# Loading convolution taps one by one on SyncE, early x loads between batches, and embedding scalings on ScalarE in a two-layer graph kernel

## The chip, the core and the metric

The kernel runs on one core of a Trainium2 chip, in one launch. The metric is the device time of that launch in microseconds. A core has TensorE (PE: matrix products, with weight loads shown as PEld), VectorE (DVE), ScalarE (ACT), GpSimd (POOL) and SyncE (SP). Each runs its own instructions in order, and waits on semaphores for the others. Transfers are issued from SP, ACT or POOL and are carried out by 16 DMA engines.

## What is computed

`x` is 128 x 128 x 256 (batch, node, channel), `adj` 128 x 128 x 128, all float32. Two layers, each added to its input:

```python
# layer 0
h = relu(layernorm(x))
hc = relu(bn1(conv1x1(h)))
x_conv = relu(bn2(conv17(hc)) + h)            # 17 taps along the nodes, 256 -> 256 channels
s = h @ w_se.T + b_se                         # embedding, 3 wide
A = exp(-dist(s, s)) * adj
x_nmp = A @ relu(h @ w_msg.T + b_msg)
x = x + gru(concat(x_conv, x_nmp), h)
# layer 1, on the first 25 nodes
h = relu(layernorm(x))
norm_w = softmax(fusion_w)                    # 5 groups of nodes
for g, idx in enumerate(GROUPS):
    out_g = graph_conv(graph_conv(h[:, idx], adj_g, W1[g], b1[g]), adj_g, W2[g], b2[g])
    fused[:, idx] += norm_w[g] * out_g
x = x + fused
```

## The kernel before

The batch of 128 is cut into 32 quads of four matrices. The 17-tap convolution is done in a frequency domain: stage a (`stage_a`, lines 368 to 419) loads a quad of x, normalises it, transposes it (`hTa`), does the 1x1 convolution (`pc`) and the forward transform (`pf`) into `X`; stage b (line 478 on) multiplies the 40 frequencies of 64 matrices by transformed weights `wf`; stage c (line 658 on) transforms back and does the gated unit. Stages a and b run once for each of two batches of 16 quads. Stage c runs over all 32 quads, together with layer 1.

The transformed weights come from the taps. `load_taps(n)` (lines 427 to 434) loads a quarter of `conv2_w` into a buffer `wt` (two of these): tap t of the quarter's rows goes to the partitions t, 32 + t, 64 + t and 96 + t. `tap_weights` (lines 436 to 463) multiplies by a constant (`pw`), copies into `ws` and stores to `wfd` in DRAM from POOL. This runs beside stage a of the first batch. The quarter n + 1 is loaded while quarter n is worked on, at its first step (for n = 0 at its fourth), and a new load waits for the buffer's last reader on TensorE.

x quads are loaded by SP in `load_x` (line 360, four transfers of 128 KB), into four buffers `xa`; the statistics (`st`, line 267, `mv`, line 268) and the normalisation (line 275) follow on VectorE, with a power on POOL (line 270) between. SP also loads the tap quarters, the late constants (`load_late`, lines 250 to 253), `wf`, and later everything that stage c reads.

Beside stages a and b, from the end of `tap_weights` on, `early(q)` works out the neighbour part of quad q (`neighbours`, line 575 on): the embedding (`pse`), four scalings of it into `ef` (lines 586 and 589), their product `lr`, the messages (`pm`), the adjacency (`pd`, `aT`) and the sum (`px`). In the second batch, `fold_gates` (lines 305 to 326) loads and combines the gate weights.

Layer 1 (`setup_1`, `rows`, `prepare`, `block`) works in eight blocks of 16 matrices. The end of a block is `turn` (transpose back), `gather` (the second adjacency product) and `fuse` (the weighted sum over groups by the matrix `s2w`, added to `x1`), for four quads each; then four stores on POOL (line 1094).

The order of all instructions is fixed when the program is built: the pieces are generators, and an `Order` picks the lane with the least work done for its weight. A `yield a, b` says that the piece did `a` us of TensorE work and wants `b` us before its next step. No engine reorders at run time.

Of the kernel before, what the change touches and what calls it, by code (L numbers as in the profile page):

```python
# [9 lines left out]
FP = mybir.dt.float32  # L10
AF = mybir.ActivationFunctionType
ALU = mybir.AluOpType
# [195 lines left out]
def kernel(ctx: ExitStack, tc: tile.TileContext, x, adj, consts, vecs, w_se, conv1_w,  # L208
# [24 lines left out]
    def c(name):  # L233
        a, b = CAT[name]
        return cst[:, a:b]
# [13 lines left out]

    def load_late():  # L250

        nc.sync.dma_start(out=wse, in_=w_se.rearrange("(k p) o -> p k o", p=P))
        nc.sync.dma_start(out=cst[:, CFIRST:], in_=consts[:, CFIRST:])

    scl, sft = {}, {}
    brz = cp.tile([P, 4], FP, name="brz")
    wse9 = wp.tile([P, 2, WIDE], FP, name="wse9")
# [70 lines left out]
    def fold_embedding():  # L328
# [9 lines left out]
                                       op0=ALU.mult, op1=ALU.add)  # L338
        yield 1.5, 0.0

    lab, turn = ExitStack(), []
# [24 lines left out]
    def stage_a(q):  # L368
        ab = LATE["ab"]
        for n in range(q, min(q + 2, (q // BQ + 1) * BQ)):  # L370
            if n not in XA:
                load_xa(n)
                if n == q:
                    yield 0.0, 14.0 if q > BQ else 6.0
        if q not in MOM:
            MOM[q] = moments(XA[q], "a")
            yield 0.0, 3.0
            normalize(XA[q], XA[q], *MOM[q])
            yield 0.0, 2.0
# [12 lines left out]
        nc.gpsimd.dma_start(out=hTd[q], in_=hT)  # L392
        h1 = ab.tile([P, GB, D], FP, tag="h1", name=f"h1{q}")
        for h in range(2):
            pc = ptmp.tile([P, 2, D], FP, tag="tmp", name=f"pc{q}_{h}")
            for i in range(2):
                for k in range(2):
                    nc.tensor.matmul(pc[:, i], hT[:, k, (2 * h + i) * N:(2 * h + i + 1) * N],  # L398
                                     c1w[:, k], start=(k == 0), stop=(k == 1))
            s = slice(2 * h, 2 * h + 2)  # L400
            nc.vector.tensor_tensor(h1[:, s], pc, brow[:, None, :].to_broadcast([P, 2, D]),
                                    ALU.add)
            nc.scalar.activation(h1[:, s], h1[:, s], AF.Relu)
            yield 1.75, 2.8 * h
        for h in range(2):
            for k in range(2):
                pf = ptmp.tile([P, 2, D], FP, tag="tmp", name=f"pf{q}_{k}_{h}")
                for i in range(2):
                    nc.tensor.matmul(pf[:, i, :F * NB], h1[:, 2 * h + i, k * P:(k + 1) * P],  # L409
                                     fwd, start=True, stop=True)  # L410
                g0 = (q % BQ * GB + 2 * h) * NB
                dst = X[:, k, :, g0:g0 + 2 * NB].rearrange("p f (g b) -> p f g b", b=NB)
                src = pf[:, :, :F * NB].rearrange("p g (f b) -> p f g b", b=NB)
                if (k, h) == (0, 0):
                    nc.vector.tensor_copy(dst, src)  # L415
# [10 lines left out]

    def load_taps(n, *engines):

        wt = tw.tile([P, 16, D], FP, tag="wt", name=f"wt{n}")
        src = conv2_w.rearrange("(r n i) t o -> n t r i o", r=4, n=4)[n]  # L430
        for r in range(4):
            engines[r % len(engines)].dma_start(out=wt[32 * r:32 * r + 16], in_=src[:16, r])
        engines[0].dma_start(out=wt[16::32], in_=src[16])
        wts.append(wt)

    def tap_weights():

        yield 0.0, 16.0
        for n in range(4):
            for m in range(8):  # L440
                if m == (0 if n else 3) and n < 3:
                    load_taps(n + 1, nc.sync, nc.gpsimd)
                if (n, m) == (2, 4):
                    load_late()
                if m % 2 == 0:
                    ws = tw.tile([P, 4, 4, D], FP, tag="ws", name=f"ws{n}_{m}", bufs=3)
# [21 lines left out]
        LATE["wn"] = wg.tile([P, 7, 2, P], FP, name="wn")  # L468
        LATE["wh"] = wg.tile([P, 7, 1, P], FP, name="wh")
        LATE["io"] = near.enter_context(tc.tile_pool(name="io", bufs=2, reuse_waits="tile"))  # L470
        LATE["fr"] = near.enter_context(tc.tile_pool(name="fr", bufs=1, reuse_waits="tile"))
        LATE["wmsg"] = LATE["fr"].tile([P, 2, D], FP, name="wmsg")
        LATE["bmsg"] = LATE["fr"].tile([P, D], FP, name="bmsg")
# [4 lines left out]
    def stage_b(bat):  # L478
# [29 lines left out]
        for f in range(NF + 1):  # L508
            if f + 3 <= NF:
                load_w(f + 3)  # L510
            if f < NF:
                add(f + 1)
            y = xf.tile([P, 2, D], FP, tag="y", name=f"y{bat}_{f}")
            pa = pgat.tile([P, 2, D], FP, tag="gat", name=f"pa{bat}_{f}")
            for s in range(2):
# [59 lines left out]
    def neighbours(q, hT, ad, xm):  # L575
# [6 lines left out]
                                 hT[:, k, j * N:(j + 1) * N], start=(k == 0), stop=(k == 1))  # L582
        ef = LATE["fr"].tile([P, 4, N], FP, tag="ef", name=f"ef{q}")
        for i in range(4):
            if i % 2 == 0:
                nc.vector.tensor_scalar(ef[:, i], pse[:, :N], emb[:, i:i + 1], embb[:, i:i + 1],
                                        op0=ALU.mult, op1=ALU.add)
            else:
                nc.scalar.activation(ef[:, i], pse[:, :N], AF.Identity, scale=emb[:, i:i + 1],
                                     bias=embb[:, i:i + 1])  # L590
        lr = LATE["fr"].tile([P, 2, N], FP, tag="lr", name=f"lr{q}")
        nc.vector.tensor_tensor(lr, ef[:, 0::2], ef[:, 1::2], ALU.mult)
        yield 0.5, 0.0
# [277 lines left out]
    def setup_1():  # L871
# [6 lines left out]
            tc.tile_pool(name="l2", bufs=2, reuse_waits="tile"))  # L878
        b2s = pool.tile([NG, D], FP, tag="dd", name="b2s")
        nc.sync.dma_start(out=b2s, in_=b2)  # L880
        fus = pool.tile([P, NG], FP, name="fus")
        nc.sync.dma_start(out=fus, in_=fusion_w.partition_broadcast(P))
        for n in range(2):
            load_w1(n)
        S["w2"] = weight(pool, W2, [P, 5, 4, D], "g (k p) o -> p g k o", "w2", nc.sync)
# [4 lines left out]
        for t in (*r4, S["yz"][:, 0], S["yz"][:, 1], S["b1"]):  # L890
            nc.gpsimd.memset(t, 0.0)
            yield 0.0, 4.0

        fmx = pool.tile([P, 1], FP, name="fmx")
        nc.vector.reduce_max(fmx, fus, axis=mybir.AxisListType.X)
        nc.vector.tensor_scalar(fus, fus, fmx, None, op0=ALU.subtract)  # L896
        nc.scalar.activation(fus, fus, AF.Exp)
        fsm = pool.tile([P, 1], FP, name="fsm")
        nc.vector.reduce_sum(fsm, fus, axis=mybir.AxisListType.X)
        nc.vector.reciprocal(fsm, fsm)  # L900
        nc.vector.tensor_scalar(fus, fus, fsm, None, op0=ALU.mult)
        nc.vector.tensor_mul(fus, fus, c("grp"))
        wrow = pool.tile([P, 1], FP, name="wrow")
        nc.vector.reduce_sum(wrow, fus, axis=mybir.AxisListType.X)
        s2w = S["s2w"] = pool.tile([P, 2 * WIDE], FP, name="s2w")
        nc.vector.tensor_scalar(s2w, c("s2"), wrow, None, op0=ALU.mult)
# [95 lines left out]
    def block(blk):  # L1002
        while not (blk in P_DONE and blk - 1 in B1_DONE):
            yield 0.0, 0.5
        pool, yz, b2row, s2w = S["pool"], S["yz"], S["b2row"], S["s2w"]
        w2, ac, r4 = S["w2"], S["ac"][blk % 2], S["r4"][blk % 2]

        for q in range(QS):
# [48 lines left out]
        def turn(q):  # L1057
            pz = ptmp.tile([P, 2, D], FP, tag="tmp", name=f"pzt{blk}_{q}")
            for a in range(2):
                for cc in range(2):  # L1060
                    b0 = q * GB + 2 * a
                    nc.tensor.transpose(
                        pz[:, a, cc * P:(cc + 1) * P],
                        yz[:, cc, b0:b0 + 2, :].rearrange("p s r -> p (s r)"), ident)
            zt = zts[q] = pool.tile([P, 2, D], FP, tag="zt", name=f"zt{blk}_{q}", bufs=3)
            nc.scalar.activation(zt, pz, AF.Copy)

        def gather(q):
# [10 lines left out]
        def fuse(q):  # L1079
            zt = zts.pop(q)  # L1080
            pf = ptmp.tile([P, D], FP, tag="tmp", name=f"pfu{blk}_{q}")
            for a in range(2):
                nc.tensor.matmul(pf[a * 2 * WIDE:(a + 1) * 2 * WIDE], s2w, zt[:, a],
                                 start=True, stop=True)
            nc.vector.tensor_add(x1[:, q], x1[:, q], pf)

        for what, q in ((turn, 0), (turn, 1), (turn, 2), (gather, 0), (gather, 1), (fuse, 0),
                        (turn, 3), (gather, 2), (fuse, 1), (gather, 3), (fuse, 2), (fuse, 3)):
            what(q)
            if (what, q) == (gather, QS - 1):  # L1090
                B1_DONE.add(blk)
            yield {turn: 0.45, gather: 0.9, fuse: 0.5}[what], 0.5
        for j in range(GB):
            nc.gpsimd.dma_start(
                out=out[blk * SB:(blk + 1) * SB, :WIDE].rearrange("(q j) n c -> j n q c", j=GB)[j],
                in_=x1[j * WIDE:(j + 1) * WIDE])
        F_DONE.add(blk)


# [5 lines left out]
    load_xa(2)  # L1105
    fold()
    beside = Lane([tap_weights()] + [early(q) for q in range(NQ)])
    gates = Lane([fold_gates()], weight=0.5)
    for bat, (during_a, during_b) in enumerate(((0.66, 0.5), (0.2, 0.65))):
        if bat:  # L1110
            take_turn("ab", 2, reuse_waits="tile")
# [58 lines left out]
```

## Time and profile before

| | us |
|---|---|
| median of three runs (2089.95 to 2099.69) | 2099.61 |
| the profiled execution, its own time | 2107.02 |
| the span in its trace | 2105.2 |
| stage a, first batch, with the tap weights | 0 to about 180 |
| stage b, first batch | about 210 to 372 |
| stage a, second batch | about 372 to 530 |
| stage b, second batch | about 535 to 707 |
| stage c and layer 1 | about 710 to 2105 |

The page gives busy time by engine, the span in forty slices, the transfer queues, the chain of work that ended last, the costliest groups and the transfers. Windows give the same busy times for any stretch. Of the transfers that matter here the list says:

```profile
xa<-in_x SPq DMA_DIRECT2D x128, 128.0 KB, 5.2
...
wt<-in_conv_w SPq DMA_DIRECT2D x8, 256.0 KB, 9.5
wt<-in_conv_w POOLq DMA_DIRECT2D x8, 256.0 KB, 11.8
...
wt<-in_conv_w SPq DMA_DIRECT2D x3, 64.0 KB
```

The columns are tile and source, issuing queue, count, size of one, and the median time from issue to landing. A quarter of the taps is four transfers of 256 KB and one of 64 KB, and SP and POOL share them.

### The profile page before, as it was taken

The numbers are of one execution on the slowest core, as the hardware profiler recorded it, in microseconds if no ns is written. First come the engines' busy times: TensorE is split into PE (matmuls) and PEld (weight loads), VectorE is DVE, ScalarE is ACT, GpSimd is POOL, SyncE is SP. The second block draws the span as 40 slices with busy tenths as digits, with TensorE's granted clock in tenths as the row PEclk, the third lists the DMA queues.
The fourth block names the chain that finished last, engine by engine and source line by source line (L and its number), as shares of the span: only waits on it lengthen the run. The fifth ranks groups of instructions, "written<-read, shape, count | busy, mean of one in ns | idle before, by whom it ended". The sixth has DMA issues, their size and how long they took to land.

```text
span 2105.2 us, 31050 instructions
## 1 busy us (share of the span) xinstructions
PE 2045.2 (97%) x11316; PEld 1657.3 (79%) x11316; DVE 1181.8 (56%) x2775; ACT 686.8 (33%) x1543; POOL 725.5 (34%) x902
## 2 busy tenths in 40 slices
PE   7978999999999999999999999999999999999998
PEld 5656888789888788787878877878787787878875
DVE  6754544786544455655654565565565655654642
ACT  4643222344222333323232232232233223223333
POOL 3432666232565222503322233224323323233230
PEclk9989999999999999999999999999999999999999
DMA  9977778744777634222323332323232333223121
GB/s 217 276 227 231 240 266 264 211 153 143 250 258 257 210 111 141 75 78 73 89 71 92 87 83 72 88 71 91 75 96 73 79 91 93 78 81 98 31 79 51
DMA packets 186870, 281.67 MB, mean 134 GB/s; under 512 B 20745, under 2 KB 139982, under 8 KB 186718
## 3 DMA queue, kind: packets, MB, share of 16 engines
q1 hardware_dynamic: 156270, 185.00, 31.0%
q0 software_dynamic: 30160, 94.46, 14.1%
q8 instruction: 90, 1.47, 0.3%
q14 instruction: 62, 0.51, 0.1%
q10 hardware_dynamic: 288, 0.22, 0.0%
HBM read 187.34 MB, written 92.27 MB: 133 GB/s over the span
## 4 chain that ended last, share of the span: by engine, by line
PE 91%; DMA 4%; DVE 2%; issue 1%; POOL 1%; ACT 0%; SPq 0%; POOLq 0%; DVEq 0%; ACTq 0%
PE p L709 41%; PE pa L502 7%; PE pm L601 5%; PE ph L1031 5%; PE pz L1040 5%; PE pc L398 4%; PE pb L502 3%; PE pi L674 3%; PE px L627 3%; PE pf L409 2%; PE pg L1074 1%; PE ph L387 1%; PE pc L688 1%; PE po L855 1%; DMA xa<-in_x 1%; PE py L1014 1%
## 5 line engine op out<-in xcount | busy, mean ns | idle before, releaser
L835 POOL TENSOR_TENSOR d<-hTc,r 128x512 f32<-128x512 f32 x64 | 81.3, 1271 | 370.9 <-ACT r L832 370.9
L502 PE MATMUL pa<-wf,X 128*128 128x256 f32 x640 | 152.5, 381 | 0.0
L864 POOL DMA_DIRECT2D out<-xt x128 | 71.9, 567 | 211.0 <-DVE xt L861 205.4
L525 DVE SCALAR_TENSOR_TENSOR y<-pa,kk 128x512 f32<-128x512 f32 x78 | 53.8, 690 | 147.0 <-ACT kk L524 147.0
L398 PE MATMUL pc<-c1w,hTa 128*128 128x256 f32 x512 | 125.4, 392 | 6.6 <-DVE X L415 4.3
L709 PE MATMUL p<-th,wrz 128*128 128x256 f32 x512 | 131.7, 380 | 0.0
L724 ACT ACTIVATE z<-z,brz 128x256 f32<-128x256 f32 x128 | 58.1, 501 | 225.5 <-DVE z L781 191.2
L709 PE MATMUL p<-tc,wrz 128*128 128x256 f32 x512 | 131.6, 380 | 0.0
L709 PE MATMUL p<-tm,wrz 128*128 128x256 f32 x512 | 131.5, 380 | 0.0
L502 PEld LDWEIGHTS pa<-wf,X 128*128 128x128 f32 x640 | 118.3, 190 | 16.2 <-issue 2.2
L601 PE MATMUL pm<-wmsg,hT 128*128 128x256 f32 x512 | 124.4, 389 | 0.0
L691 DVE SCALAR_TENSOR_TENSOR xc<-pc,s_bn,hTc 128x256 f32<-128x256 f32 x128 | 53.1, 478 | 118.3 <-PE pc L688 118.3
L398 PEld LDWEIGHTS pc<-c1w,hTa 128*128 128x128 f32 x512 | 96.0, 195 | 25.9 <-DVE X L415 4.5
L601 PEld LDWEIGHTS pm<-wmsg,hT 128*128 128x128 f32 x512 | 97.9, 194 | 16.7 <-issue 1.8
L1031 PE MATMUL ph<-yz,w 128*128 128x96 f32 (+3 forms) x640 | 109.2, 325 | 0.9 <-DVE yz L1016 0.9
L1033 ACT ACTIVATE hh<-ph,vec 128x96 f32<-128x96 f32 (+3 forms) x160 | 64.0, 402 | 134.2 <-PE ph L1031 124.7
L709 PEld LDWEIGHTS p<-tm,wrz 128*128 128x128 f32 x512 | 97.5, 190 | 13.0
L1040 PE MATMUL pz<-hh,w 128*128 128x96 f32 (+3 forms) x640 | 107.3, 322 | 0.0
L1031 PEld LDWEIGHTS ph<-yz,w 128*128 128x128 f32 x640 | 88.1, 193 | 21.9 <-issue 13.2
L709 PEld LDWEIGHTS p<-tc,wrz 128*128 128x128 f32 x512 | 95.2, 190 | 12.0 <-issue 0.5
L709 PEld LDWEIGHTS p<-th,wrz 128*128 128x128 f32 x512 | 94.9, 190 | 12.1 <-DVE fus L896 0.3
L709 PE MATMUL p<-hTc,wrz 128*128 128x256 f32 x384 | 103.9, 394 | 0.0
(204 smaller groups left out, 4562.0 us busy)
## 6 DMA issues: line engine op xcount, KB each, us to landing
wf<-wfd SPq DMA_DIRECT2D x160, 256.0 KB, 4.1
wfd<-ws POOLq DMA_DIRECT2D x64, 320.0 KB, 8.2
yd<-y POOLq DMA_DIRECT2D x80, 256.0 KB, 3.8
yt<-yd SPq DMA_DIRECT2D x64, 320.0 KB, 4.9
w<-in_W SPq DMA_DIRECT2D x40, 512.0 KB, 3.7
xa<-in_x SPq DMA_DIRECT2D x128, 128.0 KB, 5.2
hTd<-hTa POOLq DMA_DIRECT2D x32, 512.0 KB, 5.8
hT<-hTd SPq DMA_DIRECT2D x32, 512.0 KB
```

Source lines behind the costliest of these rows:

```text
L398: nc.tensor.matmul(pc[:, i], hT[:, k, (2 * h + i) * N:(2 * h + i + 1) * N], c1w[:, k], start=(k == 0), stop=(k == 1))
L502: nc.tensor.matmul(ps, xk(k), WF[f][:, k, s], start=(k == 0), stop=(k == 1))
L601: nc.tensor.matmul(pm[:, i], hT[:, k, j * N:(j + 1) * N], LATE["wmsg"][:, k], start=(k == 0), stop=(k == 1))
L627: nc.tensor.matmul(px[:, dc, i], msgs[h][:, i, dc * P:(dc + 1) * P], aT[:, 2 * h + i], start=True, stop=True)
L674: nc.tensor.matmul(pi[b * 64:(b + 1) * 64], inv[:F], yt[:, b::2], start=True, stop=True)
L709: nc.tensor.matmul(ps[:, m], w[:, i, k, m * P:(m + 1) * P], factor(i, x, t), start=first and j == 0, stop=last and j == len(n) - 1, skip_g ...
L724: nc.scalar.activation(dst[:, m], src[:, m], AF.Sigmoid, bias=brz[:, b + m:b + m + 1])
L835: nc.gpsimd.tensor_sub(d, hT[:, dc], r[:, dc])
L864: nc.gpsimd.dma_start(out=out[q * GB + j, WIDE:].rearrange("(t n) c -> n t c", n=WIDE), in_=xt[j * WIDE:(j + 1) * WIDE, 1:4])
L1031: nc.tensor.matmul(ph, w1[:, k, m * P:(m + 1) * P], yz[:, k, :, o:o + n], start=(k == 0), stop=(k == 1))
L1033: nc.scalar.activation(hh[:, m], ph, AF.Relu, bias=v("b1", g * 4 + m))
L1040: nc.tensor.matmul(pz, w2[:, g, m, cc * P:(cc + 1) * P], hs[g][:, m], start=(m == 0), stop=(m == 3))
```

## The change

It has six parts. Taps: the second, third and fourth quarter are loaded as 17 transfers of 64 KB, one for each tap, all on SP; the first quarter keeps its form. The late constants are loaded in the second quarter instead of the third, with the fusion weights ahead of them. Joint: near the end of stage b of the first batch, the first three x quads of the second are loaded into three buffers of their own (`xe`), and the first of them is normalised there; the stage a of quads 17 and 18 waits longer in the planned order. Embedding: all four scalings are done by ScalarE. Fusion weights: their softmax moves from `setup_1` to a piece after `fold_gates`. Blocks: `turn`, `gather` and `fuse` are in another order with four buffers `zt` instead of three, and the stores follow each `fuse`: one on POOL in the first seven blocks, four on SP (for the last quad two on SP, two on ACT) in the last.

```diff
 def load_late():
+        nc.sync.dma_start(out=fus, in_=fusion_w.partition_broadcast(P))
         nc.sync.dma_start(out=wse, in_=w_se.rearrange("(k p) o -> p k o", p=P))
         nc.sync.dma_start(out=cst[:, CFIRST:], in_=consts[:, CFIRST:])
...
+    def fold_fusion():
+        fmx = cp.tile([P, 1], FP, name="fmx")
+        nc.vector.reduce_max(fmx, fus, axis=mybir.AxisListType.X)
+        nc.vector.tensor_scalar(fus, fus, fmx, None, op0=ALU.subtract)
+        nc.scalar.activation(fus, fus, AF.Exp)
+        yield 0.0, 4.0
...
+        nc.vector.tensor_scalar(s2w, c("s2"), wrow, None, op0=ALU.mult)
+        yield 0.0, 0.0
...
         if q not in MOM:
+            if BQ < q < BQ + 3:
+                yield 0.0, 11.0 * (q - BQ) - 10.0
             MOM[q] = moments(XA[q], "a")
...
     def load_taps(n, *engines):
         wt = tw.tile([P, 16, D], FP, tag="wt", name=f"wt{n}")
         src = conv2_w.rearrange("(r n i) t o -> n t r i o", r=4, n=4)[n]
-        for r in range(4):
-            engines[r % len(engines)].dma_start(out=wt[32 * r:32 * r + 16], in_=src[:16, r])
-        engines[0].dma_start(out=wt[16::32], in_=src[16])
+        if n == 0:
+            for r in range(4):
+                engines[r % len(engines)].dma_start(out=wt[32 * r:32 * r + 16], in_=src[:16, r])
+        for t in range(16 if n == 0 else 0, TAPS):
+            engines[0].dma_start(out=wt[t::32], in_=src[t])
         wts.append(wt)
...
                 if m == (0 if n else 3) and n < 3:
-                    load_taps(n + 1, nc.sync, nc.gpsimd)
-                if (n, m) == (2, 4):
+                    load_taps(n + 1, nc.sync)
+                if (n, m) == (1, 3):
                     load_late()
...
+        LATE["xe"] = near.enter_context(tc.tile_pool(name="xe", bufs=1, reuse_waits="tile"))
...
+            if f >= NF - 6 and f % 3 == 0 and bat + 1 < NBAT:
+                n = (bat + 1) * BQ + (f - NF + 6) // 3
+                XA[n] = LATE["xe"].tile([P, 4, D], FP, name=f"xa{n}")
+                load_x(XA[n], n)
+            n = (bat + 1) * BQ
+            if f == NF - 3 and n in XA:
+                MOM[n] = moments(XA[n], "a")
+            if f == NF - 1 and n in XA:
+                normalize(XA[n], XA[n], *MOM[n])
...
         for i in range(4):
-            if i % 2 == 0:
-                nc.vector.tensor_scalar(ef[:, i], pse[:, :N], emb[:, i:i + 1], embb[:, i:i + 1],
-                                        op0=ALU.mult, op1=ALU.add)
-            else:
-                nc.scalar.activation(ef[:, i], pse[:, :N], AF.Identity, scale=emb[:, i:i + 1],
-                                     bias=embb[:, i:i + 1])
+            nc.scalar.activation(ef[:, i], pse[:, :N], AF.Identity, scale=emb[:, i:i + 1],
+                                 bias=embb[:, i:i + 1])
...
-            zt = zts[q] = pool.tile([P, 2, D], FP, tag="zt", name=f"zt{blk}_{q}", bufs=3)
+            zt = zts[q] = pool.tile([P, 2, D], FP, tag="zt", name=f"zt{blk}_{q}", bufs=4)
...
             nc.vector.tensor_add(x1[:, q], x1[:, q], pf)
-
-        for what, q in ((turn, 0), (turn, 1), (turn, 2), (gather, 0), (gather, 1), (fuse, 0),
-                        (turn, 3), (gather, 2), (fuse, 1), (gather, 3), (fuse, 2), (fuse, 3)):
+            b0 = blk * SB + q * GB
+            if blk < NBLK - 1:
+                nc.gpsimd.dma_start(out=out[b0:b0 + GB, :WIDE], in_=x1[:, q])
+                return
+            for j in range(GB):
+                eng = nc.scalar if q == QS - 1 and j % 2 else nc.sync
+                eng.dma_start(out=out[b0 + j, :WIDE], in_=x1[j * WIDE:(j + 1) * WIDE, q])
+
+        for what, q in ((turn, 0), (turn, 1), (turn, 2), (gather, 0), (turn, 3), (gather, 1),
+                        (gather, 2), (fuse, 0), (gather, 3), (fuse, 1), (fuse, 2), (fuse, 3)):
...
-        for j in range(GB):
-            nc.gpsimd.dma_start(
-                out=out[blk * SB:(blk + 1) * SB, :WIDE].rearrange("(q j) n c -> j n q c", j=GB)[j],
-                in_=x1[j * WIDE:(j + 1) * WIDE])
...
-    gates = Lane([fold_gates()], weight=0.5)
+    gates = Lane([fold_gates(), fold_fusion()], weight=0.5)
```

More of the change, by code (lines that the diff above doesn't have):

```diff
@@ L250, in load_late @@
     def load_late():
+        nc.sync.dma_start(out=fus, in_=fusion_w.partition_broadcast(P))
         nc.sync.dma_start(out=wse, in_=w_se.rearrange("(k p) o -> p k o", p=P))
         nc.sync.dma_start(out=cst[:, CFIRST:], in_=consts[:, CFIRST:])
+    fus = cp.tile([P, NG], FP, name="fus")
+    s2w = cp.tile([P, 2 * WIDE], FP, name="s2w")
     scl, sft = {}, {}
@@ L339, in fold_embedding @@
         yield 1.5, 0.0
+    def fold_fusion():
[4 more added lines that the diff above has]
+        yield 0.0, 4.0
+        fsm = cp.tile([P, 1], FP, name="fsm")
+        nc.vector.reduce_sum(fsm, fus, axis=mybir.AxisListType.X)
+        nc.vector.reciprocal(fsm, fsm)
+        nc.vector.tensor_scalar(fus, fus, fsm, None, op0=ALU.mult)
+        yield 0.0, 4.0
+        nc.vector.tensor_mul(fus, fus, c("grp"))
+        wrow = cp.tile([P, 1], FP, name="wrow")
+        nc.vector.reduce_sum(wrow, fus, axis=mybir.AxisListType.X)
+        nc.vector.tensor_scalar(s2w, c("s2"), wrow, None, op0=ALU.mult)
+        yield 0.0, 0.0
     lab, turn = ExitStack(), []
@@ L880, in setup_1 @@
         nc.sync.dma_start(out=b2s, in_=b2)
-        fus = pool.tile([P, NG], FP, name="fus")
-        nc.sync.dma_start(out=fus, in_=fusion_w.partition_broadcast(P))
         for n in range(2):
@@ L892, in setup_1 @@
             yield 0.0, 4.0
[L894 to L906, printed above, removed]
         b2row = S["b2row"] = pool.tile([P, D], FP, name="b2row")
@@ L1004, in block @@
             yield 0.0, 0.5
-        pool, yz, b2row, s2w = S["pool"], S["yz"], S["b2row"], S["s2w"]
+        pool, yz, b2row = S["pool"], S["yz"], S["b2row"]
         w2, ac, r4 = S["w2"], S["ac"][blk % 2], S["r4"][blk % 2]
```

## The prediction

> **What bounds the kernel now.** I read the page's shares and its forty slices first, then the table of windows over the opening 180 us, the joint between the batches and the tail, then the waits, the chain, the order of the transfers on SP and the transfers by window.
>
> ```profile
> PE 2045.2 (97%) x11316; PEld 1657.3 (79%) x11316; DVE 1181.8 (56%) x2775; ACT 686.8 (33%) x1543; POOL 725.5 (34%) x902
> ...
> PE   7978999999999999999999999999999999999998
> ```
>
> TensorE is busy for all but 60 us of the 2105.2 us span. So an edit can only win back part of these 60 us, while it can lose any amount. The windows say where they lie:
>
> ```profile
> 20.00:58.00 38.00, 38.00 (x222) 26.84 (x221) 26.32 (x68) 21.27 (x46) 13.34 (x21) 0.96 1.04 253
> 58.00:90.00 32.00, 31.50 (x199) 21.10 (x196) 24.59 (x67) 21.05 (x45) 15.91 (x24) 1.00 1.05 284
> 90.00:140.00 50.00, 39.03 (x217) 25.19 (x216) 26.53 (x68) 23.57 (x50) 18.54 (x29) 0.86 0.86 245
> ...
> 390.00:400.00 10.00, 7.10 (x49) 5.16 (x48) 8.72 (x26) 3.39 (x7) 2.22 (x4) 0.97 0.78 232
> ...
> 2090.00:2100.00 10.00, 6.53 (x50) 2.85 (x46) 4.26 (x8) 3.43 (x6) 1.10 (x3) 0.97 0.00 0
> ```
>
> Read each row as: window, length, then the busy time of PE, PEld, DVE, ACT and POOL, the granted clock, the busy share of the DMA engines, and GB/s. From 20 to 90 us TensorE loses half a microsecond, but the transfer engines show a share above 1, so the opening stage lives at the edge of its transfers. From 90 to 140 us it falls over that edge: 11 us of TensorE are lost. A wait (total, times, longest) and the chain (start, length) name the cause:
>
> ```profile
> DVE st L267 <- DMA xa<-in_x: 14.3, 3, 9.6
> ```
>
> ```profile
> 90.09 18.91 DMA wt<-in_conv_w
> 109.44 2.10 SPq L360
> 111.99 2.32 SPq L360
> 114.36 20.09 DMA xa<-in_x
> ```
>
> A tap load takes 18.91 us to land, the x load behind it on SP's queue can't be issued before, and then needs 20.09 us itself. Tap loads ahead of x loads on SP are the weak spot, and this is what the change touches. The SP order of these:
>
> ```profile
> 26.29 1.31 SPq L432 DMA_DIRECT2D wt<-in_conv_w  x2
> 27.77 0.69 SPq L433 DMA_DIRECT2D wt<-in_conv_w  x1
> 29.30 13.46 SPq L360 DMA_DIRECT2D xa<-in_x  x8
> 58.33 1.27 SPq L432 DMA_DIRECT2D wt<-in_conv_w  x2
> 59.65 0.65 SPq L433 DMA_DIRECT2D wt<-in_conv_w  x1
> 60.40 10.18 SPq L360 DMA_DIRECT2D xa<-in_x  x12
> 89.73 3.39 SPq L432 DMA_DIRECT2D wt<-in_conv_w  x2
> 93.16 1.16 SPq L433 DMA_DIRECT2D wt<-in_conv_w  x1
> 94.43 9.94 SPq L360 DMA_DIRECT2D xa<-in_x  x4
> ```
>
> Each quarter costs SP three instructions, and x follows within 5 us. L433 is the interesting one: it loads a single tap (64 KB to 4 partitions), which is the form that all 17 taps of a quarter take in the changed kernel.
>
> **What the skill says.** The Trainium skill's "DMA: Bandwidth & Descriptors", section "Why a DMA increments its semaphore by 16 and not by 1", says that a transfer runs on the largest number of engines up to 16 that divides the slowest dimension of both sides, that a transfer from SP takes the lowest-numbered ones, and that the missing counts are written at once. A single tap has the slowest dimension 4. The trace agrees: the semaphore of the L433 issued at 27.77 us gets one count at 28.88 us and only four later ones, at 37.17, 37.58, 37.88 and 38.12 us, where a 256 KB load gets sixteen. So each single tap goes over 4 engines, and if the page is right always the same four; the trace doesn't number engines. The same page's "Queues, rings and completion order" says that an engine takes turns between its queues. The trace fits: while POOL's queue is full (102 to 137 us), SP's loads need 12 to 20 us.
>
> **Taps.** A quarter has 17 x 64 = 1088 rows of 1 KB. Before, 1024 of them went 64 to an engine, and the 64 of the last tap 16 to each of four: 80 rows on the fullest engine. Now it is 1088 / 4 = 272 rows. What is a row's price? The shortest and commonest x row takes 46 ns in the transfer records, but in the stretch of tap loads (61 to 68 us) the median of the 1 KB rows is 118 ns. Landings say the same: the two 256 KB loads of 58.33 and 58.68 us, 16 rows to an engine each, landed at 63.62 and 65.52 us, 1.9 us apart; the single tap behind them was complete at 67.69 us, another 2.2 us, and its first engine at 66.41. I take 1.9 us for one tap of 16 rows on its four engines, so 17 x 1.9 = 32 us for a quarter, with bounds 12.5 us (272 x 46 ns) and 37 us (17 x 2.2). Quarters are 31 us apart (58.33 to 89.73), so the four engines would do little else. The issues themselves (17 x 0.65 = 11 us on SP) lie inside that.
>
> What is queued behind? SP's loads use eight semaphores in turn, and each load waits for the landing of the eighth before it (in the records each SP load waits for its own semaphore). So the x load behind a quarter is issued when most of the 17 taps have landed, and its own rows on these four engines come after them. Add 3 us for it (x needs about 3 to 5 us in quiet stretches), and 2 us to start. First quarter: the x already queued lands at 34.4 us, so 34.4 + 32 + 3 = 69.4 us for the x quad first used at 58.9 us: 10.5 us late. Second: 58.3 + 2 + 32 + 3 = 95.3 against its use at 78.6: 17 us. Third: 89.7 + 37 = 126.7 against 115.5: 11 us, which takes the place of the 11 us lost now rather than adding to it. The taps themselves are needed at the next quarter, 31 us after their issue, so they are no later than x. VectorE waits in order for x at L267 and queued behind it are the h1 additions and tap copies that free TensorE's PSUM banks, so TensorE stops within microseconds, as it did at 131 us. Sum: 10.5 + 17 + 11 - 11 = 27.5 us, plus about 2.5 us for the lower clock after two more stops (0.81 to 0.85 in the windows from 110 to 130 us): +30 us. Bounds: with 12.5 us a quarter nothing is late and the present 11 us go, -11; with 37 us and POOL's stores (28 rows of 4 KB at 159 ns, 4.5 us of each 9.6 us quad) taking turns on the same four engines, about +60.
>
> Moving w_se, constants and the fusion weights from 104 us to the second quarter moves 0.5 MB out of the third stall into the second window: zero in sum, within 2 us. Taking six loads off POOL saves it 6 x 0.6 us; POOL isn't what TensorE waits for there.
>
> **The joint between batches.** Three x quads of batch 1 are loaded and the first normalised during the end of stage b. From 370 to 400 us TensorE loses 5.1 us (1.3, 0.9 and 2.9), and from 420 to 450 us 2.8 us with VectorE at 8 to 9 tenths. Moments (4 x 0.6 us) and normalisation (4 x 0.4 us) of one quad leave that stretch for one where VectorE is half idle. I take -5, bounds -8 and 0.
>
> **Embedding on ScalarE.** 64 VectorE operations of 0.408 us go, 64 of 0.457 us come to ScalarE, which is at 33%. The chain before was 2 x 0.41 + 2 x 0.46 us with hand-overs, now it is 4 x 0.46: equal. The messages' products (3.7 us of TensorE) cover it; without them it would be 0.1 us a quad. In batch 1's stage a it frees 12 x 0.41 = 4.9 us of the loaded VectorE, of which TensorE waited 4.1 us (pc and pf on ef). I count -1 beyond the joint, bounds -4 and +2.
>
> **Fusion weights and tail.** The hoisted chain is 1.8 us of VectorE, and TensorE waited 0.3 us for it. In the last block the four POOL stores (2.17 us of issue after the last addition at 2098.6 us) become two each on SP and ACT, about 0.9 us, and the turn of the last quad moves ahead of gathers 1 and 2, about 1 us. I take -3, bounds -4 and 0. Earlier blocks are covered by stage c, where TensorE is at 99 to 100%.
>
> **Sum.** +30 - 5 - 1 - 3 = +21 us on the profiled 2107.02 us: 2128. That execution was 7.4 us above the median of the runs, so on the median 2099.61 + 21 = 2121 us.
>
> **Rivals.** *Four engines are quick enough, and SP alone is the better path* (the not-slower side). If a tap row costs near 46 ns instead of 118, a quarter clears in 12.5 us, before x is needed, and the 11 us stall of 90 to 140 us goes too, because x no longer lies behind 256 KB bursts and POOL's half. That gives -11 - 9 = -20: 2080 us. It decides where a quarter clears in under about 15 us (20.3 us of lead less 5), so about 55 ns a row. For it: short rows are the commonest at other times; against: the 118 ns rows are tap rows.
> *The two cancel.* At about 80 ns a row a quarter takes 22 us: the first quarter is in time, the second 6.7 us late, the third 1.3, instead of 11; with some turns lost to POOL about +8 in all, less 9: about 2099 us, no change. For it: 79 ns is the median of the first 10 us.
> *Full collision.* Taps at 37 us, with POOL's stores in turn: +60 - 9 = +51: 2150 us. For it: DMA share above 1 already; against: POOL stops producing while TensorE is stopped, so the queue empties by itself.
>
> **Numbers.** Forecast (+10 to +40) 0.49, full collision 0.16, cancel 0.19, quick engines 0.16. About 0.5% (10 us) is what a measurement of this kernel can tell from no change: its three runs span 9.7 us. So slower 0.65, same 0.19, faster 0.16. The range reaches into both outer cases, 2086 to 2155; about 0.12 is left below and 0.07 above. As cases of both signs count, the likeliest one's own range is 2110 to 2140.
>
> **What would show it.** Right: between 20 and 150 us TensorE's idle time grows from 11.5 us to about 39; st waits for x total 40 us or more; the taps on SP stretch to 25 us or more for 17 issues, and x follows them that much later; the DMA share in these windows falls although TensorE waits, since twelve of sixteen engines are free. The joint's loss near zero, ef on VectorE gone, the last stores on SP and ACT. Wrong: a tap quarter that lands within 15 us of its first issue; or x loads that land before st wants them; or an opening stage that ends before 180 us, when the total must be below 2100.

## The result and the profile after

| kernel | median us | runs | ratio to the kernel before | 95% interval |
|---|---|---|---|---|
| before | 2096.74 | 7 (2089.79 to 2099.69) | | |
| after | 2106.62 | 7 (2105.93 to 2108.36) | 1.0061 | 1.0041 to 1.0081 |

The change makes the kernel slower by 0.6%, 9.9 us by the medians and 12.8 us by the ratio (8.6 to 17.0 by its interval). Forecast were 2121 us and slower. The time lies inside the whole range of 2086 to 2155 us, but 3 us below the likeliest case's own 2110 to 2140. Of the 14.4 us between forecast and result, 2.9 are the kernel before itself, whose median over seven runs is lower than over the first three. The profiled executions can't be subtracted from each other: that of before took 2107.02 us, 10 us above its median, that of after 2108.36. Read stage by stage they are of use. A second profile of the kernel before, below, shows how far two executions of one kernel differ.

Divided at the end of the first batch's stage b, the two profiles hold the same numbers of products in each part. The kernel before comes first, then the kernel after (columns as in the prediction):

```profile
0.00:368.00 368.00, 334.51 (x2001) 262.63 (x2002) 204.46 (x479) 138.28 (x314) 174.85 (x237) 0.96 0.84 246
368.00:2105.20 1737.20, 1710.73 (x9316) 1394.70 (x9314) 977.29 (x2296) 548.55 (x1230) 550.65 (x665) 0.99 0.37 110
```

```profile
0.00:384.30 384.30, 339.94 (x2001) 265.36 (x2002) 203.66 (x470) 144.78 (x335) 173.79 (x232) 0.94 0.80 238
384.30:2106.60 1722.30, 1703.32 (x9316) 1390.40 (x9314) 959.55 (x2242) 569.01 (x1276) 554.06 (x661) 0.99 0.37 111
```

So up to there the change loses 16.3 us against this profile, and behind it wins 14.9 us: 7.5 us of idle time of TensorE and 7.4 us of busy time for the same products.

The windows of the opening, for the kernel after:

```profile
20.00:58.00 38.00, 36.82 (x225) 25.65 (x225) 26.22 (x68) 21.75 (x46) 12.04 (x19) 1.00 0.84 233
58.00:90.00 32.00, 29.09 (x159) 19.66 (x157) 15.89 (x41) 17.61 (x38) 11.80 (x16) 0.89 0.74 225
90.00:140.00 50.00, 33.26 (x186) 21.68 (x184) 23.32 (x60) 17.52 (x36) 15.16 (x22) 0.83 0.74 223
```

TensorE now loses 2.9 us in the second window and 16.7 us in the third, at a lower granted clock (0.89 and 0.83), and the DMA share has gone from 1.05 and 0.86 to 0.74 in both. More waiting for transfers with less transfer work in flight is what one would expect of a load confined to a few engines. The landing records show it directly. The semaphore of each of the 51 single taps gets one update at the issue and four later ones. The first x load behind a quarter, issued at 47.39 us, has twelve of its sixteen counts by 52.03 us; the other four come at 55.28, 56.46, 58.76 and 61.69 us, around the end of the taps (60.29 us). So the taps and a part of each x load share the same four engines. The wait view of the first 220 us, VectorE only, has one line for it (total, times, longest):

```profile
DVE st L270 <- DMA xa<-in_x: 31.0, 4, 12.9
```

It was 14.3 us in three waits. SP's order of transfers shows where x stands (start, length, engine and line, tile, count; L459 is the single tap, L381 the x load):

```profile
26.87 19.75 SPq L459 DMA_DIRECT2D wt<-in_conv_w  x17
47.39 13.22 SPq L381 DMA_DIRECT2D xa<-in_x  x8
61.77 17.78 SPq L459 DMA_DIRECT2D wt<-in_conv_w  x17
79.66 6.49 SPq L381 DMA_DIRECT2D xa<-in_x  x4
...
106.74 17.75 SPq L459 DMA_DIRECT2D wt<-in_conv_w  x17
125.31 29.19 SPq L381 DMA_DIRECT2D xa<-in_x  x20
```

In each quarter x is issued 18 to 21 us after the first tap, where it was 2 to 5 us. The chain of waits in that stretch goes from x load to x load:

```profile
53.07 11.27 DMA xa<-in_x
...
83.17 12.49 DMA xa<-in_x
...
130.06 11.03 DMA xa<-in_x
```

By the landing records, the x quads behind the three quarters were complete at 64.3, 96.6 and 141.1 us, and `st` began within 0.2 us of each. From the first tap's issue to the last tap's landing a quarter took 33.4, 31.3 and 32.8 us; before, its SP part took 9.4 to 19.3 us.

The second stage a is shorter than before: from the last product of stage b to its last `pc` it is 140.2 us instead of 162.0. But two of the quads of the neighbour part that were worked on there (6.5 before, 4.5 after, counted by the products `pm`) now run later, so this length alone says little; the division above, with equal numbers of products, is the fair comparison. The stretch from the start of the last product of the kernel (`pfu`) to the end is 7.2 us instead of 7.5.

### The profile page after: what moved, and what is told of

It is laid out like the page before. It is cut to its first block, busy times and chain, and to the rows that moved or that the text cites. A ratio compares the mean times of both kernels' runs of the same rounds, so it can differ in the third digit from the quotient of the medians.

```text
span 2106.6 us, 31107 instructions
## 1 busy us (share of the span) xinstructions
PE 2043.3 (97%) x11316; PEld 1655.8 (79%) x11316; DVE 1163.2 (55%) x2711; ACT 713.8 (34%) x1611; POOL 727.9 (35%) x892
## 4 chain that ended last, share of the span: by engine, by line
PE 89%; DMA 6%; DVE 2%; SPq 1%; issue 1%; POOL 0%; ACT 0%; DVEq 0%; POOLq 0%; ACTq 0%
PE p L741 42%; PE pa L529 7%; PE pm L633 5%; PE ph L1047 5%; PE pz L1056 5%; PE pc L421 3%; PE pb L529 3%; PE pi L706 3%; DMA xa<-in_x 3%; PE px L659 3%; PE pf L432 2%; DMA wt<-in_conv_w 2%; PE pg L1090 2%; PE po L887 1%; PE pc L720 1%; PE ph L410 1%
## 5 line engine op out<-in xcount | busy, mean ns | idle before, releaser
L756 ACT ACTIVATE z<-z,brz 128x256 f32<-128x256 f32 x128 | 58.1, 501 | 226.7 <-DVE z L813 193.0
```

The lines of the kernel that those rows point to most:

```text
L756: nc.scalar.activation(dst[:, m], src[:, m], AF.Sigmoid, bias=brz[:, b + m:b + m + 1])
```

## The experiments

Each time is the median of its runs; ratios are against runs of the kernel before on the same chip in the same session, whose medians were 2094.54 (e1 to e4), 2093.82 (e5 to e7) and 2092.72 us (e8, e9). "Stage a ends" means the start of its last `pc` in the first batch: 177.7 us before, 195.9 us after. Two theories of the loss were set against each other. *Four engines*: a single tap has four partitions, its rows run on four engines, and a quarter of 272 rows there takes 30 us, with x behind it. *SP's queue*: it is the number of transfers, their eight semaphores and POOL's half now on SP, on however many engines.

**Taps undone, and taps alone.** In `e1_taps_back` only the taps of the change are undone:

```diff
-        if n == 0:
-            for r in range(4):
-                engines[r % len(engines)].dma_start(out=wt[32 * r:32 * r + 16], in_=src[:16, r])
-        for t in range(16 if n == 0 else 0, TAPS):
-            engines[0].dma_start(out=wt[t::32], in_=src[t])
+        for r in range(4):
+            engines[r % len(engines)].dma_start(out=wt[32 * r:32 * r + 16], in_=src[:16, r])
+        engines[0].dma_start(out=wt[16::32], in_=src[16])
...
-                    load_taps(n + 1, nc.sync)
+                    load_taps(n + 1, nc.sync, nc.gpsimd)
```

> The changed kernel with the tap quarters loaded as before (four transfers of 256 KB and one of 64 KB, half of them on POOL). Taps theory (both forms: four engines, or SP's queue): the first stage a ends near 178 us again instead of 195.9, and the time falls by about 17 us to 2090 us, 7 us below the kernel before. Rival (the opening is late for another reason, such as the constants that now load in the second quarter): stage a still ends after 190 us and the time stays near 2106 us.

Measured: 2076.91 us, ratio 0.9915 (0.9893 to 0.9936). The opening's windows:

```profile
58.00:90.00 32.00, 31.46 (x196) 21.07 (x195) 24.58 (x67) 20.72 (x45) 16.21 (x24) 1.00 1.05 291
90.00:140.00 50.00, 48.75 (x291) 32.35 (x290) 35.68 (x93) 29.88 (x65) 24.34 (x36) 1.00 0.95 293
```

TensorE runs nearly without a stop, and stage a ends at 163.9 us. So without the taps the change wins 17.8 us (0.85%), twice what I had added up, and the taps cost 1.0061 / 0.9915 = 1.0147, 30.7 us, with an uncertainty of some 6 us from the two intervals. The profiles put it where it belongs: up to the end of the first stage b e1 takes 352.8 us and the change 384.3, behind it 1721.7 and 1722.3.

`e2_taps_only` makes the same edit the other way round, in the kernel before.

> The kernel before with only the tap loads changed. Taps theory: first stage a ends near 196 us, time about 2097 + 17 = 2114 us. Rival (the loss needs the other parts of the change): first stage a ends before 183 us, time within 5 us of the kernel before.

Measured: 2119.41 us, ratio 1.0118 (1.0095 to 1.0141), stage a ends at 193.0 us. The taps alone cost 24.7 us (19.9 to 29.5); the loss doesn't need the other parts.

**Number of engines.** `e3_17_on_16_engines` and `e9_17_on_8_engines` keep 17 transfers of 64 KB a quarter, all on SP at the same place, and cut them differently:

```diff
-        if n == 0:
-            for r in range(4):
+        for r in range(4):
+            if n == 0:
                 engines[r % len(engines)].dma_start(out=wt[32 * r:32 * r + 16], in_=src[:16, r])
-        for t in range(16 if n == 0 else 0, TAPS):
-            engines[0].dma_start(out=wt[t::32], in_=src[t])
+                continue
+            for i in range(0, 16, 4):
+                engines[0].dma_start(out=wt[32 * r:32 * r + 16, i:i + 4], in_=src[:16, r, i:i + 4])
+        engines[0].dma_start(out=wt[16::32], in_=src[16])
```

For eight engines the inner loop (`for i in range(0, 16, 4)` and its body) is instead

```diff
...
+            for t in (0, 8):
+                for i in (0, 8):
+                    engines[0].dma_start(out=wt[32 * r + t:32 * r + t + 8, i:i + 8],
+                                         in_=src[t:t + 8, r, i:i + 8])
```

> The changed kernel, each quarter still 17 transfers of 64 KB on SP, but sixteen of them cut so that they have 16 partitions (tap) as the slowest dimension, and so run on sixteen engines. Four-engines theory: a quarter's 17 land within 15 us, x isn't late, first stage a ends before 182 us and the time is as with the old taps, 2089 to 2094 us. SP-queue theory (17 transfers through eight semaphores ahead of x, and POOL's half added to SP): stage a still ends after 190 us, time 2102 to 2108 us.

> As e3_17_on_16_engines (17 transfers of 64 KB a quarter, all on SP, same rows), but cut so that the slowest dimension is 8 partitions, with 144 rows of a quarter on the fullest engine instead of 272 on four engines and 80 on sixteen. Four-engines theory: between the two: ratio to the kernel before 0.995 to 1.001, 2084 to 2096 us, x late by less than half of the change's 31 us of waits. SP-queue theory: no difference between 4, 8 and 16 (already hard to hold after e3).

| form | quarters, first issue to last landing, us | wait of st for x, us | ratio | 95% interval |
|---|---|---|---|---|
| 4 engines (after) | 33.4, 31.3, 32.8 | 31.0 | 1.0061 | 1.0041 to 1.0081 |
| 8 engines (e9), 2082.36 us | 23.0, 22.2, 18.1 | 9.6 | 0.9948 | 0.9932 to 0.9964 |
| 16 engines (e3), 2081.57 us | 19.8, 21.2, 17.9 | 6.8 | 0.9935 | 0.9915 to 0.9955 |
| few transfers, half on POOL (e1) | 12.4, 9.3, 16.9 (SP's part) | 7.1 | 0.9915 | 0.9893 to 0.9936 |

For e3 and e9 the wait lines of VectorE in the first 220 us are these, in that order:

```profile
DVE st L270 <- DMA xa<-in_x: 6.8, 2, 5.9
```

```profile
DVE st L270 <- DMA xa<-in_x: 9.6, 2, 8.6
```

In the records, sixteen transfers of a quarter get one update and eight later ones in e9, and sixteen later ones in e3, as the two forms intend. Same count, size, queue and place: only the cut differs, and some 26 of the 30.7 us go with it (1.0061 / 0.9935 = 1.0127). This decides for the four engines. The cut also changes which rows of the source one transfer reads together, and no run holds that fixed. But the records of the 1 KB rows don't speak for that: a row takes 65 to 70 ns on average in three stretches of taps of the change, and 75 to 89 ns in three of e3. What is left of SP's queue is 0.2% with overlapping intervals. My "within 15 us" for a quarter on sixteen engines was too good: it takes 18 to 21 us. Eight engines are nearly as good as sixteen: x is late in both, by 9.6 and 6.8 us of waits.

**Order instead of engines.** `e4_taps_spread` keeps the single taps and their four engines, and issues them three at a time (four in the first quarter) at the steps of a quarter. `load_taps` then only makes the buffer:

```diff
-        for t in range(16 if n == 0 else 0, TAPS):
-            engines[0].dma_start(out=wt[t::32], in_=src[t])
+            engines[0].dma_start(out=wt[16::32], in_=src[16])
...
                     load_taps(n + 1, nc.sync)
+                    left = list(range(TAPS))
+                if n < 3 and m >= (0 if n else 3):
+                    src = conv2_w.rearrange("(r n i) t o -> n t r i o", r=4, n=4)[n + 1]
+                    for t in left[:3 if n else 4]:
+                        nc.sync.dma_start(out=wts[n + 1][t::32], in_=src[t])
+                    left = left[3 if n else 4:]
```

> The changed kernel, single taps on SP as in the change, but issued three at each of the eight steps of a quarter (four in the first) instead of all 17 at its start, so that x lies behind few of them. Four-engines theory with the order as its carrier: the four engines have the same rows to move, but x is no longer behind a whole quarter; most of the loss goes, stage a ends at 180 to 188 us, time 2092 to 2099 us. If the four engines' throughput alone decided, x or the taps would be as late as in the change: stage a after 192 us, time above 2102 us.

Measured: 2096.51 us, ratio 1.0005 (0.9989 to 1.0021), stage a ends at 180.9 us, `st` waits 12.5 us for x. It falls in the band for the order as carrier, but that is the smaller part: of 1.46 points over e1, 0.56 go by the order alone, and 0.9 stay. The trace shows what stays. Now the taps themselves come late, and TensorE's products `pw` wait for them:

```profile
103.37 2.01 PE L482 MATMUL pw<-wt,cst 17*80 17x512 f32 x8 [6.66 <-DMA xa<-in_x]
140.39 2.01 PE L482 MATMUL pw<-wt,cst 17*80 17x512 f32 x8 [3.72 <-DMA xa<-in_x]
```

The view names x as the releaser, but `pw` reads `wt`, and the last taps of these two quarters landed at 103.17 and 140.15 us, 0.2 us ahead. At 63.24 us there is a third such wait, of 3.4 us (last tap at 63.05 us). So the four engines' throughput hurts in either order: with the taps in a block x is late, with the taps spread the taps are.

**Was the old stall the kernel's own?**

> The kernel before, unchanged, for a second profile. If its first profile (2107.0 us, above all 19 timed runs but one) caught an unusual opening, its first stage a ends well before 177.7 us here and the 11 us stall between 90 and 140 us is smaller; if the stall is the kernel's own, it is there again and the opening ends within 3 us of 177.7.

Measured in the second profile of the kernel before, 2097.65 us:

```profile
58.00:90.00 32.00, 32.00 (x201) 21.73 (x199) 25.52 (x70) 21.63 (x46) 16.31 (x25) 1.00 1.04 288
90.00:140.00 50.00, 44.51 (x260) 29.28 (x259) 33.16 (x87) 26.33 (x56) 23.58 (x36) 0.93 0.93 284
```

```profile
DVE st L267 <- DMA xa<-in_x: 7.6, 2, 6.6
```

The loss between 90 and 140 us is 5.5 us here, not 11, and stage a ends at 167.7 us, not 177.7. The wait is the same, its size changes from execution to execution. The profile that I predicted from had the large size, and with it a credit of 11 us.

**Late constants.** `e5_late_only` moves them in the kernel before.

```diff
-                if (n, m) == (2, 4):
+                if (n, m) == (1, 3):
                     load_late()
```

> The kernel before with only the late constants moved from the third quarter to the second. Late theory: half a megabyte leaves the crowded third window and the stall there goes; first stage a ends near 165 us as in e1 instead of 177.7, time 2094.5 - 12 = 2082 us. Rival (my prediction's price of zero: e1's shorter opening comes from something else or from the spread of runs): time within 4 us of the kernel before.

Measured: 2093.40 us over 14 runs, ratio 0.9997 (0.9981 to 1.0013). My theory from e1's profile falls, the price of zero stands. Its own profile ends stage a at 163.2 us, but that is one execution (2090.22 us), and the kernel before has timed executions as short as 2087.57 us in the same session.

**Joint and embedding.** `e6_no_joint` is e1 without the early x quads:

```diff
-            if BQ < q < BQ + 3:
-                yield 0.0, 11.0 * (q - BQ) - 10.0
...
-            if f >= NF - 6 and f % 3 == 0 and bat + 1 < NBAT:
-                n = (bat + 1) * BQ + (f - NF + 6) // 3
-                XA[n] = LATE["xe"].tile([P, 4, D], FP, name=f"xa{n}")
-                load_x(XA[n], n)
-            n = (bat + 1) * BQ
-            if f == NF - 3 and n in XA:
-                MOM[n] = moments(XA[n], "a")
-            if f == NF - 1 and n in XA:
-                normalize(XA[n], XA[n], *MOM[n])
```

> e1_taps_back without the joint: no early x quads, no extra waits for quads 17 and 18. If the joint is worth the 5 us that I gave it: 2077 + 5 = 2082 us (bounds 2077 to 2085), and TensorE's idle time between the last product of stage b and the end of the next stage a goes from 3.6 us back to about 8. Rival (the joint carries more, since two quads of the neighbour part move out of stage a): 2086 us or more.

Measured: 2084.84 us, ratio 0.9958 (0.9940 to 0.9977); against e1 that is 0.43 points, 9 us, with an uncertainty of some 6 us from the two intervals (e1 ran in another session and on another chip). The trace doesn't put it where I had: TensorE's idle time in the second stage a is 4.2 us without the joint and 3.6 with it. These are the windows of that stage, of the kernel before, e6 and e1, and below the last two the same windows for the instructions of `pm` alone:

```profile
368.00:530.00 162.00, 154.03 (x998) 135.57 (x996) 117.25 (x322) 70.32 (x159) 44.88 (x54) 0.98 0.54 169
```

```profile
357.10:512.90 155.80, 151.62 (x998) 133.49 (x996) 114.71 (x318) 73.89 (x172) 44.95 (x54) 1.00 0.56 176
...
357.10:512.90 155.80, 24.72 (x104) 19.19 (x104) 8.83 (x13) 1.00 0.56 176
```

```profile
352.80:493.00 140.20, 136.57 (x882) 122.82 (x881) 105.14 (x288) 67.86 (x153) 43.40 (x52) 0.99 0.54 169
...
352.80:493.00 140.20, 17.01 (x72) 13.46 (x72) 6.14 (x9) 0.99 0.54 169
```

With the joint 72 instead of 104 products of `pm` run here: the planned order places two quads of the neighbour part later. The stage is 15.6 us shorter mostly because it holds less. The fair comparison is again from the end of the first stage b to the end, with 9316 products in every kernel:

| kernel | length, us | TensorE idle, us | TensorE busy, us |
|---|---|---|---|
| before, first and second profile | 1737.2, 1738.0 | 26.5, 26.0 | 1710.7, 1712.0 |
| e2, taps only | 1732.6 | 28.6 | 1704.0 |
| after | 1722.3 | 19.0 | 1703.3 |
| e1, without the taps | 1721.7 | 18.3 | 1703.4 |
| e6, e1 without the joint | 1734.1 | 21.8 | 1712.3 |
| e7 (below), e1 with the scalings split | 1728.9 | 22.4 | 1706.5 |

By idle time the joint is worth 3.5 us, of which 2.7 lie in stage c up to layer 1's first `ph`. The other 9 us between e6 and e1 are busy time of the same products. That they belong to the joint isn't shown: e2 has no joint and none of these 9 us, and the profiled execution of e6 is the slowest of its runs (2093.01 us).

`e7_ef_split` is e1 with the scalings on both engines:

```diff
         for i in range(4):
-            nc.scalar.activation(ef[:, i], pse[:, :N], AF.Identity, scale=emb[:, i:i + 1],
-                                 bias=embb[:, i:i + 1])
+            if i % 2 == 0:
+                nc.vector.tensor_scalar(ef[:, i], pse[:, :N], emb[:, i:i + 1], embb[:, i:i + 1],
+                                        op0=ALU.mult, op1=ALU.add)
+            else:
+                nc.scalar.activation(ef[:, i], pse[:, :N], AF.Identity, scale=emb[:, i:i + 1],
+                                     bias=embb[:, i:i + 1])
```

> e1_taps_back with the four embedding scalings split between VectorE and ScalarE as before. If they are worth the 1 us that I gave them: 2076 to 2080 us. Rival (the 93 us for which ScalarE waited on VectorE's scalings and the hand-overs matter): 2082 us or more.

Measured: 2081.75 us, ratio 0.9947 (0.9930 to 0.9965), 0.32 points or 6.7 us above e1 with the same uncertainty. By the medians it lies between the two expectations. The windows of the second stage a (that of e1 stands above) show 4.0 us, with the same products in it:

```profile
350.00:494.20 144.20, 137.20 (x881) 122.17 (x880) 105.29 (x297) 65.24 (x145) 43.24 (x52) 0.99 0.51 164
```

TensorE is idle 7.0 us of it, 3.6 in e1; over the whole stretch of the table it is 4.1 us more than in e1. Its waits there name the scalings twice, 0.9 and 0.5 us, and a 2.5 us wait of `pc` on `hTa` that e1 doesn't have:

```profile
PE pc L421 <- ACT hTa L412: 2.5, 1, 2.5
...
PE pf L432 <- ACT ef L623: 0.9, 1, 0.9
```

**Tail.** In the kernel after, SP issues the last block's stores in one row:

```profile
2097.11 6.91 SPq L1108 DMA_DIRECT2D out<-x  x14
```

`e8_tail_spread` is e1 with these dealt out:

```diff
-                eng = nc.scalar if q == QS - 1 and j % 2 else nc.sync
+                eng = (nc.gpsimd, nc.gpsimd, nc.sync, (nc.sync, nc.scalar)[j % 2])[q]
```

> e1_taps_back with the sixteen stores of the last block dealt out: the first two quads' on POOL, the third's on SP, the last quad's on SP and ACT in turn. In the changed kernel SP issues 14 of them one after another in 6.9 us and is the last to finish. If that is what ends the kernel, the stretch from the last product to the end goes from 6.9 us to about 5, and the time from 2077 to about 2075 us. Rival (the landing of the last store decides, not its issue): no change.

Measured: 2075.51 us, ratio 0.9916 (0.9891 to 0.9942), the same as e1. The stretch from the start of the last product to the end became longer, 8.4 us instead of 6.9, though the stores themselves are done earlier: the last one lands 4.6 us after the start of the last product, where it was 5.8 us in e1. By the instruction records, what ends the kernel now is POOL's closing instruction, a DRAIN. It runs until 2073.34 us, 3.1 us beyond the last landing (2070.28 us); in e1 the span ends 1.1 us after the last landing. So in this profile dealing out the stores did help them, and giving POOL some of them cost more than it won. Whether a dealing over SP and ACT alone would win something stays open. e1 and e8 are the fastest kernels of the study, both about 18 us below the kernel before and 31 below the change.

## Why the prediction was right

**Sign and cause.** The cause held: a single tap runs on four engines, a quarter takes about 32 us (forecast 32, measured 31.3 to 33.4), x stands behind it on SP, and VectorE's in-order wait for x stops TensorE. e3 and e9 show the number of engines as the cause. e4 shows that the order, x behind a whole quarter, carries about 0.56 of the 1.46 points; the rest comes in any order that was tried. That the taps "are no later than x" held in the change and not in e4.

**The price of a row: right on average, and partly by luck.** I took 118 ns for a tap row, from a stretch in which taps and x were mixed, and 1.9 us for a tap. The average came true (31.3 to 33.4 us for 17 taps), its make-up did not. In the change, the records of the 1 KB rows between 33 and 47 us, all of them taps, have a median of 54 ns. Where POOL moved nothing, from 117.9 to 121.7 us, three taps landed 1.24 to 1.27 us after one another, about 78 ns a row; elsewhere it was up to 3.8 us. At 1.24 us a quarter would take 21 us. The rest fits POOL's stores taking turns on the same engines, which I had kept for the upper bound alone; no run separates it.

**Taps, +30.** In the timed runs 30.7 us within the change and 24.7 us alone. The sum was right, the terms were not, and that they cancelled is luck. `st` of the three quads behind the quarters began at 64.42, 96.77 and 141.27 us, and in the first profile of before at 58.95, 78.63 and 115.47 us. So x cost 5.5 us, then 12.7 more, then 7.7 more: 25.8 us where I had 38.5. I charged the second quarter as if the first had not delayed everything, and my 5 us for start and x was too much: x landed 34.8 and 34.3 us after the second and third quarter's first issue, not 37. In return I subtracted 11 us for the stall of before. In the first profile most of that stall (a wait of 9.6 us) lies behind these quads and is saved, and by the end of the first stage b the change is 16.3 us later. In the second profile its longest wait (6.6 us) is over at 115.49 us, there is almost nothing to subtract, and the change is 26.6 us later.

**What was to be seen.** Forecast were 40 us of waits for x (31.0 came), 39 us of idle TensorE from 20 to 150 us (25.0), and 17 tap issues stretched over 25 us (17.8 to 19.8). The last has a reason in the trace: each load waits for the landing of the eighth before it, so the seventeenth is issued when the ninth has landed, well before the quarter is complete. The falling DMA share came as forecast.

**The other parts, -9: mis-sized.** This is the term that made 21 us out of what became 12.8. e1 puts it at 17.8 us. I began with "an edit can only win back part of these 60 us" of idle time. In the profiles the stretch behind the first stage b wins 14.9 us, of which 7.5 are idle time, near what I had, and 7.4 busy time of the same products, which I had at nothing. What makes this busy time vary stays open, as e2 and e6 show. Embedding on ScalarE, "I count -1 beyond the joint": the wait view showed 4.1 us of TensorE waiting for these scalings, and I gave them to the joint. e7 shows that they are their own, 4.1 us of idle time and 6.7 us in the timed runs. Joint, -5: 3.5 us of idle time and 9 us in the timed runs, with the uncertainty said above, and not where I had read it off the windows. The idle time in the second stage a was largely the embedding's: 8.0 us before, 4.2 in e6, which has the new embedding and no joint. Fusion weights and tail, -3: what e1, e6 and e7 leave of the timed runs is about 2 us, less than its uncertainty. In the profiles the last block is 1.3 us shorter (36.0 to 34.7 us from its first `ph` to its last product). I had counted two stores each on SP and ACT and left out that twelve more of the three quads before stand on SP's queue, half a microsecond each. Late constants, 0: 0.

**Rivals.** Quick engines is refuted by the quarters of 31 us and more. Full collision (+60 us for the taps) is refuted by e2's 24.7 us and by the 30.7. As its counter-argument said, POOL issued no store from 84.8 to 100.4 us and from 130.7 to 144.9 us, around the stops of TensorE. That the two cancel was near: the loss of 30.7 us exceeds the gains of 17.8 by 12.8 us, where I had 21, and 10 us was what I had called the least that can be told from no change.

## What to carry to other kernels

Before splitting a load, look at the slowest dimension that each piece keeps: 17 loads of 64 KB cost 26 us more on four engines than the same 17 on sixteen, with the same bytes, queue and place. What counts is also what is queued behind it, and how many microseconds before its use that was issued: here 20 us of lead nearly covered a quarter on sixteen or eight engines (6.8 and 9.6 us of waits), and not one on four (31.0). Spreading such a load in time is no cure by itself: in e4 its own reader then waited. And take two profiles before crediting a stall as removed: between 90 and 140 us TensorE lost 11 us in one execution and 5.5 in the other.

## What the runs showed of the hardware

A quarter cut for eight engines took 18 to 23 us, for sixteen 18 to 21, and for four 31 to 33, so the time is far from proportional to the rows on the fullest engine (144, 80 and 272). Per row on the fullest engine that is about 115 to 123 ns with four, 125 to 160 with eight, 220 to 265 with sixteen, all beside POOL's stores.

The engines that a transfer uses can be read from its semaphore: a single tap got one update and four later ones, the cut for eight engines one and eight, and the 256 KB loads sixteen. An x load behind a quarter on four engines had twelve of its sixteen counts 9.7 us ahead of the last (52.03 against 61.69 us).

POOL's closing DRAIN ended 1.1 us after the last landing in the kernel before, whose last stores are POOL's, and 3.1 us after it in e8, with eight late stores on POOL.

The kernel before spreads over 17 to 22 us from execution to execution (2087.57 to 2104.82 us in 20 runs of one session, 2086.42 to 2108.41 in 19 of another), the change over 2.4 us in 7 runs, e2 over 6.0 in 4. The two profiles of before differ by 10 us, all of it before the end of the first stage a. That an opening at the edge of its transfers varies, and one that is surely late is late by nearly the same amount each time, fits this; it wasn't tested.
